# Picking source rows two tiles at a time, with the second scores a quarter later, in a three-layer graph transformer

## The chip, the cores and the metric

The kernel runs on one core of a Trainium2 chip. The core has TensorE (matmul, "PE"; its weight loads are "PEld"), VectorE ("DVE"), ScalarE ("ACT"), GpSimd ("POOL") and SyncE ("SP", which here only issues DMAs). The engines run side by side, each working through its own instructions in order; semaphores make one wait for another. TensorE writes to PSUM, which has eight banks of 2 KB in each of 128 partitions. The metric is device time in microseconds, lower is better.

## The reference

The input is a graph of 6250 nodes with 64 features and 206,250 directed edges sorted by their end node, each with 64 features of its own. Three layers of one-head attention over the incoming edges follow one another, then a softmax and a last normalization:

```python
q = x @ Wq + bq; k = x @ Wk + bk; v = x @ Wv + bv; e = edge_attr @ We
alpha = sum(q[dst] * (k[src] + e)) / sqrt(64)
w = softmax of alpha over the edges of one dst
x = relu(segment_sum((v[src] + e) * w, dst) + x @ Ws + bs)     # layer norm after layers 0 and 1
out = layernorm(x0 + log_softmax(x))
```

## The kernel before

Keys and values of a source node are linear in its features, so the kernel never builds them per edge. It brings the raw features `x[src]` of each edge next to the edge's own features, scores the 128-wide pair against a transformed query, sums the pairs with the softmax weights, and multiplies by Wv and We once per node.

Edges come in *chunks* of 768 (6 tiles of 128) whose end nodes lie within a window of 32 (`W`); four chunks make a *unit*, 67 full units and a short one. The chunks of a unit are four strips of 32 rows of one score matrix of 128 x 768. Scores, softmax and sums of a chunk go as partial results to DRAM (`tables`), and groups of four blocks of nodes are finished, as soon as their chunks are through, by a generator `finish` whose steps are advanced by `close_up`. This is the *node work*: combining the partials, the projection, the norm, and query and skip of the next layer (`project`). In layers 1 and 2 `close_up` is called in a unit's first quarter alone.

The rows `x[src]` come in two ways. Some tiles are gathered by indirect DMAs on GpSimd (line 601), released ahead of time by small copies on ScalarE (`gate`, line 633). The others are *picked* on TensorE (class `Picker`). Edges were sorted within their chunk in layer 0 so that all edges of a tile half draw from one stretch of eight blocks of nodes. A one-hot matrix (`hot`, line 1335, VectorE) picks the partition by matmul (line 1387, eight matmuls of 128x256 a tile pair; what is called a picked tile here is one tile position of two chunks, with four candidate blocks each, and fills one PSUM bank of 512 columns, tag `x`, of which there are two). Of the four candidates VectorE keeps the right one: a copy (line 1356) and three predicated copies (line 1359), `evacuate`. In layers 1 and 2 a unit has seven picked tiles, four for the first pair of chunks and three for the second, and `evacuate` is issued right behind the matmuls of its tile. `swap` (ScalarE, line 1346) exchanges the halves of a pair's tiles once all of them are there.

All five engines have a schedule written out by hand: instructions go to each engine in the order in which the code issues them. The loop over units (line 1904) goes through four *quarters* j = 0..3. In unit u the features of unit u are transposed (`turn`, lines 1679 and 1682), scores, softmax and weights of unit u-1 are made, unit u-2 is summed, and the tiles of unit u+1 are picked. In layers 1 and 2 the order is:

- before the quarters: `sums(u-2)` (line 1746, then a ScalarE copy), first half of the scores of u-1 (line 1692, bank `s`);
- quarter 0: `turn(0)`; the first maximum (`most`, line 1706, VectorE); the second half of the scores, bank `m`; one picked tile; the second maximum and behind it the exponential (line 1720, ScalarE); another picked tile; node work; requests for the queries of u+1 (line 1633, SP);
- quarter 1: `turn(1)`, two picked tiles;
- quarter 2: transposes of the first half of the probabilities (`weights`, line 1734, bank `p`, copied by line 1737), `turn(2)`, two picked tiles, transposes of the second half, the mask of u+1 and the first of its four loads of edge features (line 1659; the others follow at later turns);
- quarter 3: `turn(3)`, one picked tile, four stores of the partial results of u-2 (line 1757, SP); at the end the eight one-hot instructions for unit u+2.

The queries are written to one DRAM table `qq` (line 1442) and read from it with an offset known at run time (line 1633).

## Time and profile before

| | us |
|---|---|
| timed runs, median of 3 | 4206.91 (4202.07 to 4214.05) |
| the profiled execution | 4197.44 |
| its span, first to last instruction | 4195.7 |
| busy: PE / DVE / ACT / POOL | 3513.2 / 3452.3 / 2347.5 / 2563.3 |

In rows by line, `x7392 | 1084.9, 294` means 7392 instructions, 1084.9 us in which at least one was under way, 294 ns mean length; what follows is the idle time of the engine just before them and what ended it. Matmuls overlap one another, so the mean length is more than the distance from one to the next. In timeline rows the first number is the start in us, the second the length of a merged run of like instructions. In rows by stretch the columns are length, busy time of PE, PEld, DVE, ACT and POOL with instruction counts, the mean granted TensorE clock (1.00 is full rate), the share of the DMA engines in use, and GB/s.

### The profile page before, as it was taken

The numbers are of one execution on the slowest core, as the hardware profiler recorded it, in microseconds if no ns is written. First come the engines' busy times: TensorE is split into PE (matmuls) and PEld (weight loads), VectorE is DVE, ScalarE is ACT, GpSimd is POOL, SyncE is SP. The second block draws the span as 40 slices with busy tenths as digits, with TensorE's granted clock in tenths as the row PEclk, the third lists the DMA queues.
The fourth block names the chain that finished last, engine by engine and source line by source line (L and its number), as shares of the span: only waits on it lengthen the run. The fifth ranks groups of instructions, "written<-read, shape, count | busy, mean of one in ns | idle before, by whom it ended". The sixth has DMA issues, their size and how long they took to land.

```text
span 4195.7 us, 109920 instructions
## 1 busy us (share of the span) xinstructions
PE 3513.2 (84%) x35239; PEld 2484.7 (59%) x35239; DVE 3452.3 (82%) x12154; ACT 2347.5 (56%) x5994; POOL 2563.3 (61%) x2510
## 2 busy tenths in 40 slices
PE   3878889998998998895988888888858888888886
PEld 2445555555555555553767667666647667666674
DVE  5678898889888898874888888888758888888886
ACT  0445555655565555563655555555535656666665
POOL 5466666666666666663766666666447666666662
PEclk9899999999999999996999999999979999999998
DMA  5666666667666667665777777777648777777774
GB/s 109 177 165 180 174 186 177 175 181 187 179 176 181 178 173 183 180 182 130 189 182 183 182 176 178 192 176 182 164 127 192 185 174 185 187 179 183 179 179 101
DMA packets 779286, 729.02 MB, mean 174 GB/s; under 512 B 483080, under 2 KB 607938, under 8 KB 778704
## 3 DMA queue, kind: packets, MB, share of 16 engines
q1 hardware_dynamic: 630436, 512.79, 49.9%
q0 software_dynamic: 80000, 82.08, 10.2%
q10 hardware_dynamic: 68268, 127.03, 8.4%
q8 instruction: 288, 4.72, 0.5%
q14 instruction: 294, 2.41, 0.2%
HBM read 562.78 MB, written 158.68 MB: 172 GB/s over the span
## 4 chain that ended last, share of the span: by engine, by line


## 5 line engine op out<-in xcount | busy, mean ns | idle before, releaser
L601 POOL DMA_INDIRECT feat<-x,gate x1328 | 1318.0, 992 | 729.0 <-ACT gate L633 356.4
L601 POOL DMA_INDIRECT feat<-in_x,gate x1100 | 1172.1, 1066 | 690.4 <-ACT gate L633 369.6
L1387 PE MATMUL ps_x<-parts,hot 128*128 128x256 f32 x7392 | 1084.9, 294 | 223.1 <-DVE feat L1359 185.9
L1387 PEld LDWEIGHTS ps_x<-parts,hot 128*128 128x128 f32 x7392 | 946.0, 193 | 383.0 <-issue 213.5
L1682 ACT COPY featT<-ps_a 64x384 f32<-64x384 f32 x1588 | 753.8, 475 | 372.9 <-PE ps_a L1679 351.5
L1359 DVE COPY_PREDICATED feat<-which,ps_x 128x128 f32<-128x128 int32 x2772 | 838.0, 302 | 95.5
L1335 DVE TENSOR_SCALAR hot<-keys,rank 128x512 fp32r<-128x512 f16 (+1 forms) x1304 | 507.3, 457 | 4.7 <-DMA keys<-keyS 4.7
L1074 DVE TENSOR_SCALAR hit<-ruler,pos 128x384 bf16<-128x384 f16 x1608 | 456.3, 325 | 6.3 <-PE ps_m L1094 5.4
L1679 PE MATMUL ps_a<-ident,feat 128*128 128x128 f32 x2380 | 420.9, 286 | 40.7 <-DMA feat<-x,src_b 31.9
L1679 PEld LDWEIGHTS ps_a<-ident,feat 128*128 128x128 f32 x2380 | 279.6, 145 | 226.0 <-issue 185.3
L1356 DVE COPY feat<-ps_x 128x128 f32<-128x128 f32 x924 | 263.9, 286 | 173.6 <-PE ps_x L1387 166.4
L1692 PE MATMUL ps_s<-featT,q 128*32 128x384 f32 x2134 | 289.5, 507 | 81.4 <-DMA featT<-eaS 43.1
L1720 ACT ACTIVATE prob<-prob,part 128x768 f32<-128x768 f32 x204 | 190.3, 933 | 232.0 <-DVE part L1719 200.5
L1746 PE MATMUL ps_g<-feat,probT 128*32 128x128 f32 x9672 | 311.7, 275 | 2.4 <-ACT probT L1737 2.4
L1085 PE MATMUL ps_x<-hit,raw 128*64 128x384 bf16 x1608 | 294.5, 362 | 0.5 <-DVE hit L1074 0.4
L1746 PEld LDWEIGHTS ps_g<-feat,probT 128*32 128x32 f32 x9672 | 261.9, 110 | 25.6 <-ACT probT L1737 4.1
L1085 PE MATMUL ps_x<-hit,rest 128*64 128x384 bf16 x1608 | 276.2, 340 | 0.0
L1085 PE MATMUL ps_x<-hit,end 128*64 128x384 bf16 x1608 | 275.6, 339 | 0.0
L1737 ACT COPY probT<-ps_p 128x384 f32<-128x384 f32 x399 | 191.8, 481 | 124.7 <-PE ps_p L1734 92.8
L1734 PE MATMUL ps_p<-ident,prob 128*128 128x128 f32 x1197 | 206.8, 283 | 9.7 <-ACT prob L1720 9.6
L1118 ACT COPY eT<-ps_x 128x384 f32<-128x384 f32 x268 | 129.3, 483 | 122.1 <-PE ps_x L1085 84.7
L1136 ACT COPY feat<-ps_a 128x384 f32<-128x384 f32 x256 | 122.1, 481 | 133.6 <-PE ps_a L1128 97.4
(266 smaller groups left out, 5167.9 us busy)
## 6 DMA issues: line engine op xcount, KB each, us to landing
featT<-eaS SPq DMA_DIRECT2D x792, 192.0 KB
feat<-eaP SPq DMA_DIRECT2D x134, 768.0 KB
keys<-keyS SPq DMA_DIRECT2D x132, 448.0 KB
raw<-in_ea SPq DMA_DIRECT2D x536, 96.0 KB
eaS<-eT ACTq DMA_DIRECT2D x134, 384.0 KB
eaP<-feat ACTq DMA_DIRECT2D x128, 384.0 KB
shade<-maskS SPq DMA_DIRECT2D x198, 192.0 KB
feat<-x,gate POOLq DMA_INDIRECT x1328
```

What stands on the lines that cost most here:

```text
L601: nc.gpsimd.indirect_dma_start(out=feat[:, c, t, 0], out_offset=None, in_=xts[layer][:, :], in_offset=bass.IndirectOffsetOnAxis(ap=index[: ...
L1074: nc.vector.tensor_scalar(hit, ruler, self.pos[:, at : at + 1], None, ALU.is_equal)
L1085: nc.tensor.matmul(self.px[j * D : (j + 1) * D, :HE], self.parts[2 * h + i].thirds[part][:, j, t * D : (t + 1) * D], self.hits[h, 2 * i + ...
L1335: nc.vector.tensor_scalar(hot[:, h], keys[self.layer, k][:, first : first + n], rank[:, h : h + 1], None, ALU.is_equal)
L1356: nc.vector.tensor_copy(found, px[:, :, 0])
L1359: nc.vector.copy_predicated(found, which[:, first : first + 2, b].bitcast(I32).unsqueeze(2).to_broadcast([P, 2, D]), px[:, :, b],)
L1387: nc.tensor.matmul(px[:, v].rearrange("p b d -> p (b d)"), hot[:, h, (2 * pair + v) * P : (2 * pair + v + 1) * P], those[:, i, b0 + h * KB ...
L1679: nc.tensor.transpose(pt[:, t * P : (t + 1) * P], rows[:, 2 * t * D : 2 * (t + 1) * D], ident)
L1682: nc.scalar.copy(featT[:, :, h, :], pt[h * D : (h + 1) * D, : n * P].rearrange("d (i e) -> d i e", e=P))
L1692: nc.tensor.matmul(p_s[rows, :w], self.q[:, rows], self.featT[j][:, cols], start=True, stop=True)
L1734: nc.tensor.transpose(p_t[:, t, :n], self.prob[:n, at : at + P], ident[:n, :n])
L1746: nc.tensor.matmul(p_g[rows, :].rearrange("n (h d) -> n h d", h=2), self.probT[:, t, rows], batch[:, j, t], start=(t == 0), stop=(t == sel ...
```

## The change

In layers 1 and 2 the picked tiles are taken two positions at a time (`picks`, with a room of 2): sixteen matmuls into a PSUM tile of two adjoining banks, then one copy and three predicated copies for both. A unit has four such steps (two, two, two and one tile), one in each quarter. Two of the double tiles take four banks, so layers 1 and 2 run with a new PSUM pool: tag `s` serves the first scores and the first weights, `p` the sums, the second scores and the second weights, `a` the turns and the node work. Layer 0 keeps single tiles and its banks.

In all layers the sums of u-2 are issued in two pieces, three tiles before the first scores of u-1 and three behind, and the stores of the partial results in two halves, in quarters 1 and 3. In layers 1 and 2 the second scores are issued in quarter 1 behind `turn(1)`, and the second maximum, with the exponential, behind quarter 1's picked pair. All four loads of a unit's edge features are issued in quarter 2 of the unit before; the fourth has a buffer of its own. Query table and skip table get one copy for each layer (the skip table in the same way as `qq`). For units without a stored mask (three in layer 0 and the short one) the decoding of the mask (`uncode`) moves from the request to the third quarter of its own unit. The class `Line` learns to sum up to a given tile and to store one half.

```diff
--- before.py
+++ after.py
...
@@ -524,10 +523,17 @@
     nodes = ctx.enter_context(tc.tile_pool(name="nodes", bufs=2))
     early = ctx.enter_context(ExitStack())
     sorts = early.enter_context(tc.tile_pool(name="sorts", bufs=2))
+    psum = [early.enter_context(tc.tile_pool(name="psum0", bufs=1, space=bass.MemoryType.PSUM))]
     stock = [early.enter_context(tc.tile_pool(name="picks0", bufs=2))]
 
-    def ps(tag):
-        return psum.tile([P, 512], F32, tag=tag, name=f"ps_{tag}", bufs={"a": 2, "x": 2}.get(tag, 1))
+    bank_of = {"node": "g", "s0": "s", "s1": "s", "w0": "p", "w1": "p"}
+
+    def ps(use):
+        tag = bank_of.get(use, use)
+        wide = 2 if len(psum) > 1 and tag == "x" else 1
+        return psum[-1].tile(
+            [P, wide * 512], F32, tag=tag, name=f"ps_{tag}", bufs={"a": 2, "x": 2}.get(tag, 1)
+        )
 
     U0 = LEAD[0]
     STEP = -(-(N - WB * P) // (NW - 1))
...
@@ -697,7 +703,7 @@
     tables = [dram.tile([(NB + 1) * P, R], F32, name=f"part{h}") for h in range(2)]
     empty = const.tile([P, R], F32, name="empty")
 
-    qq = dram.tile([P, (NB + 1) * P], F32, name="qq")
+    qq = [dram.tile([P, (NB + 1) * P], F32, name=f"qq{i}") for i in range(L)]
     eps = const.tile([P, 1], F32, name="eps")
 
     def locate(k, m):
...
@@ -1351,55 +1358,65 @@
 
             if not self.late:
                 return
-            k, pair, t, px, which = self.late.pop()
-            found = loaded[self.layer, k][:, 2 * pair : 2 * pair + 2, t, 0]
-            nc.vector.tensor_copy(found, px[:, :, 0])
-            first = t * LB + 2 * pair
+            k, pair, t, m, px, which = self.late.pop()
+            found = loaded[self.layer, k][:, 2 * pair : 2 * pair + 2, t : t + m, 0]
+            which = which.rearrange("p (t c) b -> p c t b", c=LB)[:, 2 * pair : 2 * pair + 2, t : t + m]
+            px = px.rearrange("p t c b d -> p c t b d")
+            nc.vector.tensor_copy(found, px[:, :, :, 0])
             for b in range(1, KB):
                 nc.vector.copy_predicated(
                     found,
-                    which[:, first : first + 2, b].bitcast(I32).unsqueeze(2).to_broadcast([P, 2, D]),
-                    px[:, :, b],
+                    which[:, :, :, b].bitcast(I32).unsqueeze(3).to_broadcast([P, 2, m, D]),
+                    px[:, :, :, b],
                 )
-            if t == self.plan[k][pair] - 1:
-                self.swaps.append((k, pair, t + 1))
+            if t + m == self.plan[k][pair]:
+                self.swaps.append((k, pair, t + m))
 
         def flush(self):
 
             self.evacuate()
             self.swap()
 
+        def picks(self, k):
+
+            room = 2 if self.layer else 1
+            return [
+                (pair, t, min(room, most - t))
+                for pair, most in enumerate(self.plan.get(k, ()))
+                for t in range(0, most, room)
+            ]
+
         def batch(self, k):
 
-            for pair, most in enumerate(self.plan.get(k, ())):
-                for t in range(most):
-                    if not self.layer:
-                        self.swap()
-                    self.aim()
+            for pair, t0, m in self.picks(k):
+                if not self.layer:
+                    self.swap()
+                self.aim()
+                bank = "x" if self.layer else "pssp"[self.quarter]
+                px = ps(bank)[:, : m * 512].rearrange("p (t c b d) -> p t c b d", t=m, c=2, b=KB)
+                for t in range(t0, t0 + m):
                     at, hot = self.hots[k, t]
-                    bank = "x" if self.layer else "pssp"[self.quarter]
-                    px = ps(bank).rearrange("p (s b d) -> p s b d", s=2, b=KB)
                     for v in range(2):
                         w = t * WT + v
                         those, b0 = parts[w // HALF], w % HALF * WB
                         for h in range(NH):
                             for i in range(2):
                                 nc.tensor.matmul(
-                                    px[:, v].rearrange("p b d -> p (b d)"),
+                                    px[:, t - t0, v].rearrange("p b d -> p (b d)"),
                                     hot[:, h, (2 * pair + v) * P : (2 * pair + v + 1) * P],
                                     those[:, i, b0 + h * KB : b0 + (h + 1) * KB, :].rearrange("p b d -> p (b d)"),
                                     start=(h == 0 and i == 0),
                                     stop=(h == NH - 1 and i == 1),
                                 )
-                    self.late.append((k, pair, t, px, self.which[k]))
                     if not any(t < more for more in self.plan[k][pair + 1 :]):
                         self.free.append(self.hots.pop((k, t))[0])
-                    if self.layer:
-                        due = len(self.swaps)
-                        self.evacuate()
-                        self.swap(len(self.swaps) - due)
-                    self.aim()
-                    yield
+                self.late.append((k, pair, t0, m, px, self.which[k]))
+                if self.layer:
+                    due = len(self.swaps)
+                    self.evacuate()
+                    self.swap(len(self.swaps) - due)
+                self.aim()
+                yield
             self.which.pop(k, None)
 
     def late():
...
@@ -1612,6 +1629,11 @@
             self.mask = tos.tile([P, CE], BF16, name="shade")
             to = self.mask
             nc.sync.dma_start(to[:n, :], places[self.c : self.c + self.m].rearrange("c b e -> (c b) e"))
+
+        def uncode(self):
+
+            n = self.m * (BITS + 1)
+            to = self.mask
             for cols in self.halves:
                 w = cols.stop - cols.start
                 pc = ps("a")
...
@@ -1640,14 +1662,18 @@
             self.featT = []
             if not self.placed:
                 self.cover()
-            self.more()
+            for _ in range(self.m if self.layer else 1):
+                self.more()
 
         def more(self):
 
             j = len(self.featT)
             if j == self.m:
                 return
-            self.featT.append(work.tile([P, CE], F32, name="featT", bufs=6))
+            if self.layer and j == LB - 1:
+                self.featT.append(stock[0].tile([P, CE], F32, name="fourth", bufs=2))
+            else:
+                self.featT.append(work.tile([P, CE], F32, name="featT", bufs=6))
             if not self.plain:
                 self.turned(j, True)
 
...
@@ -1736,11 +1762,13 @@
                 self.probT = work.tile([P, TC, P], F32, name="probT", bufs=1)
             nc.scalar.copy(self.probT[:, t0 : t0 + m, :n], p_t[:, :, :n])
 
-        def sums(self):
-
-            p_g = ps("g")[:, :P]
+        def sums(self, first, upto):
+
+            if not first:
+                self.summed = ps("g")[:, :P]
+            p_g = self.summed
             batch = loaded[self.layer, self.k]
-            for t in range(self.tiles):
+            for t in range(first, upto):
                 for j in range(self.m):
                     rows = slice(j * W, (j + 1) * W)
                     nc.tensor.matmul(
@@ -1750,10 +1778,13 @@
                         start=(t == 0),
                         stop=(t == self.tiles - 1),
                     )
-            nc.scalar.copy(self.part[: self.rows, :P], p_g[: self.rows, :])
-
-        def store(self):
+            if upto == self.tiles:
+                nc.scalar.copy(self.part[: self.rows, :P], p_g[: self.rows, :])
+
+        def store(self, half=None):
             for j in range(self.m):
+                if half is not None and j // 2 != half:
+                    continue
                 nc.sync.dma_start(
                     tables[(self.c + j) % 2][ds(self.b[j], W), :], self.part[j * W : (j + 1) * W, :]
                 )
...
@@ -1904,13 +1947,13 @@
         for u in range(NU - 2):
             this = chunks[layer, u]
             picking = picker.batch(u + 1)
-            n = picked(layer, u + 1)
-            n //= 2
+            n = len(picker.picks(u + 1))
             pace = 0 if layer else 6 if u < 3 else 3
             while not opened:
                 move(1)
+            line.sums(u - 2, HT)
+            line.products(u - 1, 0)
             line.sums(u - 2)
-            line.products(u - 1, 0)
             if waiting:
                 active.append(waiting.pop(0))
             for j in range(LB):
@@ -1923,15 +1966,17 @@
                 free(u, j)
                 if j == 0 and layer:
                     line.most(u - 1, 0)
-                    line.products(u - 1, 1, "m")
+                if j == 1 and layer:
+                    line.products(u - 1, 1)
                 if j == 1:
+                    line.begun()
                     if not layer and placed(0, u + 1):
                         line.most(u - 1, 1)
                 a, b = -(-n * j // LB), -(-n * (j + 1) // LB)
                 if layer:
                     for i in range(max(b - a, 1)):
                         next(picking, None)
-                        if not i and not j:
+                        if not i and j == 1:
                             line.most(u - 1, 1)
                 if j == 0:
                     close_up()
@@ -1955,6 +2000,8 @@
                         chunks[layer, u + 1].across()
                 if j == 2:
                     line.weights(u - 1, 1)
+                    if not this.placed:
+                        this.uncode()
                     decode(layer, u + 2)
                     if placed(layer, u + 1):
                         chunks[layer, u + 1].across()
@@ -1980,6 +2027,8 @@
             lacking.extend(range(NW))
             if not layer:
                 early.close()
+                psum.append(ctx.enter_context(tc.tile_pool(name="psum", bufs=1, space=bass.MemoryType.PSUM)))
+                bank_of.update({"g": "p", "node": "a", "s1": "p", "w0": "s"})
                 stock[0] = ctx.enter_context(tc.tile_pool(name="picks", bufs=2))
                 parts.append(stock[0].tile([P, 2, HALF * WB, D], F32R, name="parts", bufs=1))
         u = NU - 2
...
```

74 lines of the change are left out of this document (43 added, 31 removed).

## The prediction

> **What bounds the kernel now.** I read the page first, then the busy time by stretch, the starts of one line that runs once in each unit, and the timeline of a unit without side work. Layers 1 and 2 hold what the change rewrites: the picked tiles of line 1387 and their copies.
>
> ```profile
> PE 3513.2 (84%) x35239; PEld 2484.7 (59%) x35239; DVE 3452.3 (82%) x12154; ACT 2347.5 (56%) x5994; POOL 2563.3 (61%) x2510
> ...
> L1387 PE MATMUL ps_x<-parts,hot 128*128 128x256 f32 x7392 | 1084.9, 294 | 223.1 <-DVE feat L1359 185.9
> ...
> L1359 DVE COPY_PREDICATED feat<-which,ps_x 128x128 f32<-128x128 int32 x2772 | 838.0, 302 | 95.5
> ```
>
> Over the span TensorE is busiest. Each picked unit has 56 picking matmuls (7 tiles of 8), so 7392 of them are 132 units, all in layers 1 and 2. Next, two stretches by engine (length, then busy us of TensorE, its weight loads, VectorE, ScalarE, GpSimd, then granted clock, DMA share, GB/s): one quiet unit, with no node work, and 700 us of layer 1.
>
> ```profile
> 2022.08:2035.68 13.60, 12.45 (x140) 10.44 (x140) 12.18 (x43) 8.69 (x24) 10.28 (x11) 1.00 0.79 193
> 2200.00:2900.00 700.00, 604.58 (x6149) 487.20 (x6148) 594.05 (x2076) 402.81 (x1038) 424.61 (x430) 0.98 0.73 181
> ```
>
> The quiet unit takes 13.60 us with TensorE at 12.45 and VectorE at 12.18: two engines nearly full, neither alone the bound. The softmax exponential of line 1720 runs once a unit, so its first and last starts give the mean unit:
>
> ```profile
> L1720 ACT ACTIVATE prob<-prob,part x64: 934/937/942, 2008.5 to 3012.9; 128x768 f32<-128x768 f32 x64
> ...
> L1720 ACT ACTIVATE prob<-prob,part x64: 935/937/940, 3140.6 to 4129.8; 128x768 f32<-128x768 f32 x64
> ```
>
> (3012.9-2008.5)/63 = 15.94 us in layer 1, (4129.8-3140.6)/63 = 15.70 in layer 2; mean 15.82. Now the timeline of quiet units (start, length, engine, line, operation). The reader is to see the order within each engine, and who hands over to whom.
>
> ```profile
> 2036.53 0.19 ACT L1720 ACTIVATION_READ_ACCUMULATOR prob<-prob,part 128x1 f32 x1
> ...
> 2038.03 0.49 PE L1734 MATMUL ps_p<-ident,prob 128*128 128x128 f32 x3
> ...
> 2038.60 2.29 PE L1387 MATMUL ps_x<-parts,hot 128*128 128x256 f32 x16
> ...
> 2040.72 0.49 PE L1734 MATMUL ps_p<-ident,prob 128*128 128x128 f32 x3
> ...
> 2041.30 1.19 PE L1387 MATMUL ps_x<-parts,hot 128*128 128x256 f32 x8
> ...
> 2042.42 1.52 PE L1746 MATMUL ps_g<-feat,probT 128*32 128x128 f32 x48
> 2042.53 0.29 DVE L1356 COPY feat<-ps_x 128x128 f32<-128x128 f32 x1 [0.20 <-PE ps_x L1387]
> ...
> 2042.85 0.98 DVE L1359 COPY_PREDICATED feat<-which,ps_x 128x128 f32<-128x128 int32 x3
> ...
> 2043.76 0.83 PE L1692 MATMUL ps_s<-featT,q 128*32 128x384 f32 x8
> 2043.87 2.98 DVE L1335 TENSOR_SCALAR hot<-keys,rank 128x512 fp32r<-128x512 f16 x8
> ...
> 2044.51 0.55 PE L1679 MATMUL ps_a<-ident,feat 128*128 128x128 f32 x3
> ...
> 2044.99 0.85 PE L1692 MATMUL ps_m<-featT,q 128*32 128x384 f32 x8
> ...
> 2045.77 2.16 PE L1387 MATMUL ps_x<-parts,hot 128*128 128x256 f32 x16
> ...
> 2046.77 0.54 DVE L1706 CUSTOM_DVE_ANT_0 prob<-ps_s,shade 128x384 f32<-128x384 f32 x1
> ...
> 2047.25 0.28 DVE L1356 COPY feat<-ps_x 128x128 f32<-128x128 f32 x1
> ...
> 2047.78 0.49 PE L1679 MATMUL ps_a<-ident,feat 128*128 128x128 f32 x3
> 2048.44 0.61 DVE L1706 CUSTOM_DVE_ANT_0 prob<-ps_m,shade,most 128x384 f32<-128x384 f32 x1
> ...
> 2049.28 0.94 ACT L1720 ACTIVATE prob<-prob,part 128x768 f32<-128x768 f32 x1 [1.99 <-DVE part L1719]
> ```
>
> The order is that of the code. On VectorE the second maximum (2048.44) stands right behind the copies of the first picked tile (2047.25); the exponential follows at 2049.28. In a unit's third quarter TensorE transposes its result (line 1734, at 2038.03), long after the exponential and its accumulator read ended at 2036.53+0.19 = 2036.72: three picked tiles lay between, and nobody waited. That slack is what the change spends.
>
> **The change part by part.** *Two tiles copied together.* 28 copies a unit become 16. A single tile's four take 2042.53 to 2043.83, 1.30 us. Price by element:
>
> ```profile
> L1511 DVE TENSOR_TENSOR w<-w 128x512 f32<-128x512 f32 x8 | 5.5, 692 | 0.3
> ...
> L1533 DVE TENSOR_TENSOR vb<-vb,sk 128x256 f32<-128x256 f32 x8 | 3.4, 424 | 0.3
> ```
>
> From 256 to 512 elements an instruction gains 692-424 = 268 ns, 1.05 ns an element; 128 more elements cost 134 ns. No row shows the two-bank form; it lies between no extra (1.30 us for four) and double (2.60). I take 1.30+4x0.134 = 1.83, as the copies are per-element work like those rows. VectorE then needs 3x1.83+1.30 = 6.8 instead of 7x1.30 = 9.1 us a unit: 2.3 us off VectorE. TensorE keeps its 56 matmuls.
>
> *Second scores and second maximum a quarter later.* In the second quarter the code now issues: tile transposes, second scores, 16 picking matmuls; on VectorE the pair's copies, and only then the second maximum; on ScalarE the exponential. The next thing in TensorE's queue is the third quarter's transposes of the probabilities. So from the end of the second quarter's picking TensorE stands still for the whole chain: 0.11 to the first copy (as from 2042.42 to 2042.53), 1.83 copies, 2049.28-2048.44 = 0.84 maximum to exponential, then exponential to the end of its read, 2036.72-2035.68 = 1.04 (the preceding exponential started one 13.60 us unit before 2049.28), some 0.01 more. **3.83 us, every unit.** Nothing covers it: in layers 1 and 2 node work is issued in the first quarter alone. Behind the waiting transposes are queued the third quarter's tile transposes, 16 picking matmuls and all that follows. With the copies' bounds the gap is 3.3 to 4.6 us.
>
> *The unit after.* TensorE start to start: sums 1.34 (2042.42 to 2043.76; in two pieces, the same 48 matmuls), first scores 0.75, first transposes 0.48, second transposes 0.48 the same, second scores 0.78 (2044.99 to 2045.77), three pairs at 2.06 (between 2.01 at 2045.77 and 2.12 at 2038.60) = 6.18, probabilities and tile transposes 0.57 (2038.03 to 2038.60) and 0.58 (2040.72 to 2041.30), last tile 1.12. Sum 12.28; with the gap 16.11. Does VectorE hold it up elsewhere? The first pair starts 2.57 us into the unit; its first one-hot tile (two of the eight instructions that take 2.98 us from 2043.87) is ready at 2.2, the second at 2.9 when 3.6 is due: no. The first pair's copies end at 6.7, the second pair's matmuls at 7.95: no, and 1.3 us of VectorE lie free for node work. Quiet unit: **16.11 against 13.60**.
>
> *Node work and loads.* Before, a mean unit is 15.82-13.60 = 2.22 above the quiet one. After, VectorE's part of node work falls into idle time; TensorE's stays on the path. Its rows for 43 units:
>
> ```profile
> L1537 PE MATMUL ps_g<-ve,wT 128*128 128x64 f32 x64 | 9.4, 294 | 8.3 <-DVE skip L1448 8.3
> L1437 PE MATMUL ps_a<-xT,eq 64*128 64x512 f32 x16 | 9.0, 641 | 0.0
> L1446 PE MATMUL ps_g<-ws,xT 64*128 64x65 f32 x64 | 8.8, 278 | 0.0
> L1515 PE MATMUL ps_a<-ident,w 128*128 128x128 f32 x32 | 5.0, 278 | 0.0
> L1432 PE MATMUL ps_a<-ident,y 128*64 128x128 f32 x31 | 4.7, 272 | 0.0
> ```
>
> 36.9/43 = 0.86 us; I add 0.2 for clashes on the two banks these outputs now share with the tile transposes: 1.06. The loads of the edge features go out together in the third quarter of the unit before, and the query table gets one copy a layer, so these waits of the same 700 us should go, and no longer cost anything:
>
> ```profile
> PE ps_x L1387 <- DVE feat L1359: 52.1, 62, 1.8
> PE ps_s L1692 <- DMA featT<-eaS: 19.7, 13, 3.1
> ...
> SPq L1633 <- DMA qq<-qs: 48.4, 8, 6.3
> ```
>
> SP's queue keeps its number of DMAs. Half the stores move from the fourth quarter to the second; they wait for a copy of sums that are issued at the unit's start, and behind them on SP stand loads that are needed only in the next unit. GpSimd's gathers are released by copies whose place does not change.
>
> *Clock.* What does a gap of 3.83 us do to the clock? Two gaps of layer 1, and the stretches behind them:
>
> ```profile
> 2102.87 2.02 PE L1692 MATMUL ps_s<-featT,q 128*32 128x384 f32 x4 [3.70 <-DMA featT<-eaS]
> ...
> 2470.09 2.32 PE L1692 MATMUL ps_s<-featT,q 128*32 128x384 f32 x4 [2.97 <-DMA featT<-eaS]
> ```
>
> ```profile
> 2100.00:2102.87 2.87, 0.00 (x0) 0.00 (x0) 1.47 (x5) 0.00 (x0) 2.13 (x2) 0.77 0.59 127
> 2102.87:2110.00 7.13, 7.13 (x34) 3.88 (x34) 1.54 (x6) 2.09 (x6) 5.57 (x6) 0.61 0.55 137
> ...
> 2470.00:2476.00 6.00, 5.91 (x30) 2.89 (x31) 1.14 (x4) 2.09 (x6) 1.65 (x3) 0.72 0.48 94
> ```
>
> Behind 2.97 us of idle the clock was 0.72 over 6 us: 1.7 us of full clock lost. Around 3.70 us it was 0.77 already inside the gap and 0.61 over the 7.13 us behind: 2.8 lost. So 0 to 2.8 a unit (0 would need this not to recur). I take 1.8, near the smaller row, since dense picking follows my gap where single scores with 1.9 us more of waits and half-rate work followed those.
>
> The Trainium skill ("TensorE: Matmul & The Clock Gate", Part 1) has TensorE drop to half rate after one idle free-running window of about 3.4 us. By that rule alone a 3.83 us gap holds a whole window in some 12% of units, an estimate from the page of 0.2 us a unit and 4410 us in all, against 4620 by the rows. The trace goes further than the page: 2.97 us sufficed.
>
> *The rest.* Layer 0 keeps single tiles and its banks; sums around the scores reorder the same matmuls (nothing; -20 to +10 us). Layer tails share banks (a few us more) but wait less for masks: nothing, within 15.
>
> *Sum.* 16.11+1.06+1.8 = 18.97 against 15.82: +3.15 us, times 132 = +416. The profiled execution took 4197.44 (span 4195.7), 9.5 below the median 4206.91 and below the lowest timed run. Against its own time 4613; on the median's scale about **4620**.
>
> **The rivals.** *The clock stays up:* +1.35 a unit, +178: 4385. The Trainium skill's rule above would put the time beside this case. For it: gaps follow dense work. Against: both gaps above.
>
> *The clock is lost as behind the 3.70 us gap:* 2.8 instead of 1.8, +132 more: 4755. For: its length is the nearest to 3.83. Against: there TensorE went on in single scores.
>
> *Faster: the gap doesn't form.* If the second maximum did not stand behind the second pair's copies, its 0.84 and the exponential's 1.04 would hide behind 2.06 us of picking; then a unit is 12.28+1.06 = 13.34, -2.48, times 132 = -327: 3880. For: VectorE's lighter load is real, 52.1 us of TensorE's waits in that stretch are for these copies. Against: the code issues copies first, and the timeline shows VectorE taking a maximum only after the copies issued before it. It decides below 2.48 us of gap and lost clock together.
>
> **How the numbers follow.** Gap with about one clock loss (4480 to 4720): 0.6; clock stays up: 0.18; larger loss: 0.12; no gap: 0.08; gains and losses meet: 0.02. The likeliest gives 4620. The range, 4370 to 4770, takes in both clock cases. Slower by over 0.3% (13 us, about what this measurement can tell): 0.90; within: 0.02; faster: 0.08.
>
> **What would show it.** Right: 396+132 = 528 copies of one kind; a TensorE wait on the exponential before line 1734's transposes near 3.8 us in nearly every unit of layers 1 and 2, ScalarE's exponential starting behind a maximum that starts behind the pair's last predicated copy; a quiet unit of 17 to 18 us; a granted clock under 0.9 in both layers; VectorE's busy time down by about 260 us; the waits for edge features and for the query table gone; layer 0 unchanged. Wrong: exponential ended before the second pair's last matmul; clock at 0.97 or more; a pair's copies far from 1.83 us.

## The result and the profile after

Over four executions each, on the same chip, the changed kernel takes 4529.35 us (4525.71 to 4531.18) and the kernel before 4210.48 us (4202.07 to 4223.55). The ratio is 1.0761 [1.0735, 1.0787]: slower by 7.6%. The forecast was 4620 us with a range of 4370 to 4770. The profiled execution of the changed kernel took 4530.92 us, with a span of 4529.2, against 4197.44 before: 333 us more.

From the page of the changed kernel: busy time by engine, the granted TensorE clock in 40 slices, and three groups (line, engine, operation, tiles, count | busy us, mean ns | idle us before them and its releaser).

```profile
PE 3617.2 (80%) x35239; PEld 2688.7 (59%) x35239; DVE 3214.5 (71%) x10570; ACT 2366.7 (52%) x5994; POOL 2578.6 (57%) x2510
...
PEclk9899999999999999978888888888788888888887
...
L1365 DVE COPY feat<-ps_x 128x256 f32<-128x256 f32 (+1 forms) x528 | 202.8, 384 | 839.6 <-PE ps_x L1404 837.0
...
L1367 DVE COPY_PREDICATED feat<-which,ps_x 128x256 f32<-128x256 int32 (+1 forms) x1584 | 649.4, 410 | 54.3
L1760 PE MATMUL ps_s<-ident,prob 128*128 128x128 f32 (+1 forms) x417 | 112.6, 401 | 533.2 <-ACT prob L1746 533.2
```

VectorE's busy time fell from 3452.3 to 3214.5 us, and its share from 82% to 71%, as the joint copies were to do. TensorE issues the same 35239 instructions, but its share fell from 84% to 80%, and from the 18th slice on, where layer 1 begins, the clock is at 7 or 8 tenths where it was mostly at 9. One group holds the idle time: the transposes of the probabilities (line 1760) waited 533.2 us for ScalarE's exponential of line 1746. The predicated copies (line 1367), the largest VectorE group, still take 649.4 us, in 1584 instructions. The clock and the transposes in the kernel before, for comparison:

```profile
PEclk9899999999999999996999999999979999999998
...
L1734 PE MATMUL ps_p<-ident,prob 128*128 128x128 f32 x1197 | 206.8, 283 | 9.7 <-ACT prob L1720 9.6
```

The waits of TensorE between 2200 and 2900 us (engine, tile and line, what it waited for: us in total, times, longest), where before the copies of picked tiles and the loads of edge features headed the list; its first line is now

```profile
PE ps_s L1760 <- ACT prob L1746: 146.1, 37, 4.7
```

The copies and the loads are no longer among the waits, and 146.1/37 = 3.95 us a unit stands in their place. Now one quiet unit of the changed kernel. The timeline is of its second and third quarter (start, length, engine, line, operation, in brackets the wait before it):

```profile
2039.36 0.42 DVE L1365 COPY feat<-ps_x 128x256 f32<-128x256 f32 x1 [0.93 <-PE ps_x L1404]
2039.81 1.39 DVE L1367 COPY_PREDICATED feat<-which,ps_x 128x256 f32<-128x256 int32 x3
...
2041.10 0.61 DVE L1732 CUSTOM_DVE_ANT_0 prob<-ps_p,shade,most 128x384 f32<-128x384 f32 x1
...
2041.94 0.93 ACT L1746 ACTIVATE prob<-prob,part 128x768 f32<-128x768 f32 x1 [4.20 <-DVE part L1745]
...
2042.78 0.19 ACT L1746 ACTIVATION_READ_ACCUMULATOR prob<-prob,part 128x1 f32 x1
...
2043.02 0.61 PE L1760 MATMUL ps_s<-ident,prob 128*128 128x128 f32 x3 [3.71 <-ACT prob L1746]
...
2043.92 3.43 PE L1404 MATMUL ps_x<-parts,hot 128*128 128x256 f32 x16
...
2050.97 0.55 PE L1705 MATMUL ps_a<-ident,feat 128*128 128x128 f32 x3
...
2051.28 2.14 PE L1404 MATMUL ps_x<-parts,hot 128*128 128x256 f32 x16
```

This is the chain that the prediction had worked out, link by link: picked pair, copy 0.42, three predicated copies 1.39, and only then the second maximum at 2041.10; the exponential at 2041.94, its accumulator read, and at 2043.02 the transposes, for which TensorE stood still for 3.71 us. The 16 picking matmuls that follow take 3.43 us; the next pair, at 2051.28, takes 2.14. The same place by stretch (length, busy us of TensorE, its weight loads, VectorE, ScalarE and GpSimd, then granted clock, DMA share, GB/s), with one whole quiet unit and the 700 us of layer 1 that the prediction used:

```profile
2024.66:2041.94 17.28, 13.58 (x138) 11.87 (x138) 10.45 (x30) 8.88 (x24) 12.86 (x14) 0.90 0.61 162
2043.00:2047.00 4.00, 3.98 (x21) 3.98 (x22) 0.00 (x0) 2.73 (x7) 2.56 (x4) 0.57 0.96 259
2047.00:2056.50 9.50, 9.50 (x119) 7.91 (x118) 8.03 (x23) 5.03 (x14) 7.21 (x8) 1.00 0.44 117
2200.00:2900.00 700.00, 549.78 (x5272) 476.93 (x5272) 444.54 (x1333) 350.12 (x890) 369.21 (x371) 0.86 0.61 156
```

The clock is 0.57 for the 4 us behind the gap and 1.00 again in the next 9.5 us: 4 x 0.43 = 1.7 us of full clock lost for one gap. The whole unit takes 17.28 us where it took 13.60. The mean unit comes from the exponential's first and last start in each layer:

```profile
L1746 ACT ACTIVATE prob<-prob,part x64: 934/934/936, 2007.4 to 3182.3; 128x768 f32<-128x768 f32 x64
...
L1746 ACT ACTIVATE prob<-prob,part x63: 934/934/936, 3311.1 to 4448.8; 128x768 f32<-128x768 f32 x63
```

That is (3182.3-2007.4)/63 = 18.65 us in layer 1 and (4448.8-3311.1)/62 = 18.35 in layer 2, 18.50 in the mean where it was 15.82. The 2.68 us more, over the 125 intervals counted here, are 335 us: the whole of the 333 that the profiled execution lost. Layer 0 gave and took nothing: layer 1's first counted exponential starts at 2007.4, and did at 2008.5.

### The profile page after: what moved, and what is told of

It reads as the page before. It is cut to its first block, busy times and chain, and to the rows that moved or that the text cites. A ratio compares the mean times of both kernels' runs of the same rounds, so it can differ in the third digit from the quotient of the medians.

```text
span 4529.2 us, 107247 instructions
## 1 busy us (share of the span) xinstructions
PE 3617.2 (80%) x35239; PEld 2688.7 (59%) x35239; DVE 3214.5 (71%) x10570; ACT 2366.7 (52%) x5994; POOL 2578.6 (57%) x2510
## 4 chain that ended last, share of the span: by engine, by line
## 5 line engine op out<-in xcount | busy, mean ns | idle before, releaser
L1404 PE MATMUL ps_x<-parts,hot 128*128 128x256 f32 x7392 | 1193.8, 322 | 0.0
L1404 PEld LDWEIGHTS ps_x<-parts,hot 128*128 128x128 f32 x7392 | 1096.1, 225 | 82.6 <-DVE feat L1365 43.1
L1365 DVE COPY feat<-ps_x 128x256 f32<-128x256 f32 (+1 forms) x528 | 202.8, 384 | 839.6 <-PE ps_x L1404 837.0
L1708 ACT COPY featT<-ps_a 64x384 f32<-64x384 f32 x1320 | 626.8, 475 | 169.6 <-PE ps_a L1705 154.9
L1367 DVE COPY_PREDICATED feat<-which,ps_x 128x256 f32<-128x256 int32 (+1 forms) x1584 | 649.4, 410 | 54.3
L1760 PE MATMUL ps_s<-ident,prob 128*128 128x128 f32 (+1 forms) x417 | 112.6, 401 | 533.2 <-ACT prob L1746 533.2
L1760 PEld LDWEIGHTS ps_s<-ident,prob 128*128 128x128 f32 (+1 forms) x417 | 61.9, 191 | 564.0 <-ACT prob L1746 560.5
L1774 PE MATMUL ps_p<-feat,probT 128*32 128x128 f32 x6600 | 235.8, 276 | 11.9 <-DVE most L1732 9.2
L1774 PEld LDWEIGHTS ps_p<-feat,probT 128*32 128x32 f32 x6600 | 179.7, 110 | 84.6 <-issue 50.9
L1763 ACT COPY probT<-ps_p 128x384 f32<-128x384 f32 (+1 forms) x269 | 129.3, 481 | 192.4 <-PE ps_p L1760 165.5
```

The costliest lines, as they stand in the source:

```text
L1365: nc.vector.tensor_copy(found, px[:, :, :, 0])
L1367: nc.vector.copy_predicated(found, which[:, :, :, b].bitcast(I32).unsqueeze(3).to_broadcast([P, 2, m, D]), px[:, :, :, b],)
L1404: nc.tensor.matmul(px[:, t - t0, v].rearrange("p b d -> p (b d)"), hot[:, h, (2 * pair + v) * P : (2 * pair + v + 1) * P], those[:, i, b0 ...
L1708: nc.scalar.copy(featT[:, :, h, :], pt[h * D : (h + 1) * D, : n * P].rearrange("d (i e) -> d i e", e=P))
L1774: nc.tensor.matmul(p_g[rows, :].rearrange("n (h d) -> n h d", h=2), self.probT[:, t, rows], batch[:, j, t], start=(t == 0), stop=(t == sel ...
```

## The experiments

**Theory:** the second maximum stands on VectorE behind the copies of the second quarter's pair, so exponential and transposes come one after the other behind the picking, TensorE waits 3.7 to 3.95 us in every unit, and its clock falls behind each wait. **Rivals:** the new layout of the banks makes pieces wait that did not before; steps of two tiles are too coarse, whatever their order; the clock has another cause than the wait.

The first four runs shared a chip on which the kernel before took 4203.19 us (4192.06 to 4218.63, nine executions). In the diffs, `-` is the changed kernel of this document unless another is named.

### e1: the second maximum ahead of the pair

```diff
                 if layer:
+                    if j == 1:
+                        line.most(u - 1, 1)
                     for i in range(max(b - a, 1)):
                         next(picking, None)
-                        if not i and j == 1:
-                            line.most(u - 1, 1)
```

> The second maximum is issued ahead of quarter 1's picked pair instead of behind it; all else as changed. Theory (the gap: maximum and exponential stand behind the pair's copies, and TensorE's next work needs them): the exponential now runs beside the pair's sixteen matmuls. VectorE is still busy with the first pair's copies until about 0.9 us before the second pair's matmuls end, so about 1.05 us of the gap stays in a quiet unit, too short to lose the clock as a rule: quiet unit 13.1 us, mean unit 14.2 to 14.8, total 3980 to 4080 us. Rival 1 (shared banks: sums, second scores and second weights queue for one bank): the banks are the same, so it stays at 4450 or more. Rival 2 (coarse steps: sixteen matmuls against one set of copies leave both engines idle in turn): the steps are the same, 4450 or more.

It took 4185.98 us, ratio 0.997 [0.9953, 0.9988]: one call moved ahead of a loop takes back all of the loss and a little more, with the same banks and the same steps of two tiles. So neither layout nor step is what the time was lost to. The size was missed by 100 us. A quiet unit of this run, and the stretch of layer 1:

```profile
2032.30:2045.29 12.99, 12.07 (x140) 10.33 (x138) 10.46 (x30) 8.69 (x24) 9.94 (x11) 1.00 0.78 208
2200.00:2900.00 700.00, 602.34 (x6363) 515.12 (x6354) 536.90 (x1616) 419.81 (x1077) 454.21 (x447) 0.95 0.71 187
```

The wait in that stretch:

```profile
PE ps_s L1760 <- ACT prob L1746: 88.0, 42, 4.0
```

and its exponential in layer 1 (duration, then first and last start):

```profile
L1746 ACT ACTIVATE prob<-prob,part x65: 932/935/937, 2006.4 to 2986.6; 128x768 f32<-128x768 f32 x65
```

The quiet unit is 12.99 us where 13.1 was expected, with 0.92 us of the wait left in it, and below the 13.60 of before. But over the stretch the wait is still 88.0/42 = 2.1 us and the clock 0.95, and the mean unit is (2986.6-2006.4)/64 = 15.32. VectorE's timeline in a unit with node work shows why:

```profile
2205.13 1.22 DVE L1525 TENSOR_TENSOR w<-both,mm 128x1024 f32<-128x1024 f32 x1
...
2206.38 0.69 DVE L1528 TENSOR_TENSOR w<-w 128x512 f32<-128x512 f32 x1
...
2206.99 0.61 DVE L1732 CUSTOM_DVE_ANT_0 prob<-ps_p,shade,most 128x384 f32<-128x384 f32 x1
```

The node work (lines 1525 and 1528), issued in the first quarter, now stands ahead of the second maximum in place of the copies. The prediction's rival without a gap left this out, and its 3880 us were too low for it.

### e2: the transposes later

The other end of the chain. The exponential stays late, and what waits for it moves behind the third quarter's picked pair.

```diff
-                if j == 2:
+                if j == 2 and not layer:
                     line.weights(u - 1, 0)
                 this.turn(j)
...
                 if j == 2:
+                    if layer:
+                        line.weights(u - 1, 0)
                     line.weights(u - 1, 1)
```

> Maximum and exponential stay where the change put them; the transposes of the first half of the probabilities move on TensorE from ahead of quarter 2's turn to behind its picked pair. Theory: the chain of 3.8 us runs beside the turn and sixteen matmuls (2.3 us) of quarter 2; what is left of the gap is about 1.5 us, or none where the engine lags; mean unit 14.3 to 15.2, total 4000 to 4130 us. Rivals (shared banks, coarse steps): 4450 or more.

4148.01 us, ratio 0.9875 [0.9857, 0.9892]: faster than both kernels, though 18 us above the expected range. The waits of the stretch:

```profile
PE ps_s L1760 <- ACT prob L1746: 71.1, 44, 2.1
PE ps_p L1774 <- ACT probT L1763: 46.6, 43, 1.1
```

The stretch itself:

```profile
2200.00:2900.00 700.00, 580.79 (x6303) 501.08 (x6306) 534.40 (x1598) 414.62 (x1065) 443.98 (x442) 0.99 0.71 185
```

and one quiet unit's transposes in the timeline:

```profile
2045.63 0.55 PE L1760 MATMUL ps_s<-ident,prob 128*128 128x128 f32 x3 [1.51 <-ACT prob L1746]
```

The wait for the exponential fell to 71.1/44 = 1.6 us, with the clock at 0.99. A new wait of 46.6/43 = 1.1 us stands beside it: the sums now wait for ScalarE's copies of the transposed weights, which run later too. This new wait is what the expectation had not priced in. In the quiet unit the first wait is 1.51 us, and it leaves the clock up.

### e3: the gap filled with work

Does the wait cost the clock, or something else? Thirteen matmuls of the identity with itself, written into the tile that the transposes then overwrite, fill the gap. They are useless work; the result stays the same.

```diff
+            if self.layer and not h and self.c // LB < NU - 3:
+                for _ in range(13):
+                    nc.tensor.matmul(p_t[:, 0, :], ident, ident, start=True, stop=True)
             for t in range(m):
                 at = (t0 + t) * P
                 nc.tensor.transpose(p_t[:, t, :n], self.prob[:n, at : at + P], ident[:n, :n])
```

> Thirteen matmuls of the identity with itself are put on TensorE ahead of the first transposes of the probabilities, into the same bank, which the transposes overwrite: about 3 us of work without use inside the gap. The wait for the exponential stays. Theory: granted clock in layers 1 and 2 goes from 0.86 to 0.97 or more, quiet unit from 17.3 to 15.9, total 4340 us (4310 to 4400): the clock's own share of the loss, 1.4 us a unit. If the clock is lost for another reason or does not set the time: 4500 to 4600.

4295.77 us, ratio 1.0224 [1.0189, 1.0259], a little below the expected range. A kernel with more to do is faster than the changed one. The quiet unit and the stretch:

```profile
2036.22:2051.97 15.75, 14.93 (x167) 13.23 (x165) 10.46 (x30) 8.69 (x23) 12.09 (x13) 1.00 0.73 189
2200.00:2900.00 700.00, 653.85 (x7002) 572.59 (x7001) 494.27 (x1486) 387.55 (x999) 424.05 (x414) 1.00 0.67 173
```

The chain's place in the timeline of the quiet unit and the one behind it:

```profile
2049.18 3.06 PE L1760 MATMUL ps_s<-ident 128*128 128x128 f32 x26
...
2051.97 0.94 ACT L1746 ACTIVATE prob<-prob,part 128x768 f32<-128x768 f32 x1 [4.29 <-DVE part L1745]
...
2053.05 0.55 PE L1763 MATMUL ps_s<-ident,prob 128*128 128x128 f32 x3 [0.81 <-ACT prob L1746]
...
2053.69 2.14 PE L1404 MATMUL ps_x<-parts,hot 128*128 128x256 f32 x16
...
2055.67 0.49 PE L1763 MATMUL ps_p<-ident,prob 128*128 128x128 f32 x3
```

The clock is 1.00 throughout. The chain is unchanged: from the fill's start at 2049.18 to the transposes at 2053.05 it is 3.87 us, of which 0.81 remain as a wait. So what separates this run from the changed kernel is the clock: (1.0761-1.0224) x 4210 = 226 us, over 132 units 1.7 us each, the same 1.7 that the stretch behind one gap showed. The remaining 2.2% is what the chain costs beyond what VectorE's lighter load saves.

### e5: single tiles in the new order

```diff
-            room = 2 if self.layer else 1
+            room = 1
```

> Layers 1 and 2 pick single tiles again (seven a unit: two, two, two, one in the quarters), in the changed order and banks; the second maximum stands behind quarter 1's first tile, ahead of its second. Theory: the gap is one tile's copies 1.30, maximum 0.84, exponential 1.04 and 0.1, less the second tile's matmuls 1.07: 2.2 us; TensorE 12.1+2.2 and part of the clock loss: quiet unit about 15.3, total 4290 to 4400 us. Rival 2 (coarse steps): back to the 4210 us of before or under it. Rival 1 (banks): 4450 or more.

4484.09 us, ratio 1.0672 [1.0654, 1.069]: above what was expected. What TensorE waited for in the stretch:

```profile
PE ps_s L1760 <- ACT prob L1746: 121.1, 39, 4.5
```

The transposes of one quiet unit in the timeline, with the wait ahead of them, and the picking behind:

```profile
2046.75 0.55 PE L1760 MATMUL ps_s<-ident,prob 128*128 128x128 f32 x3 [1.97 <-ACT prob L1746]
...
2047.55 3.52 PE L1404 MATMUL ps_x<-parts,hot 128*128 128x256 f32 x16
```

The 4 us behind that wait, and the stretch:

```profile
2047.00:2051.00 4.00, 4.00 (x23) 4.00 (x22) 1.21 (x4) 2.73 (x7) 3.09 (x4) 0.57 1.01 267
2200.00:2900.00 700.00, 564.26 (x5449) 481.86 (x5448) 526.11 (x1846) 363.04 (x921) 382.45 (x382) 0.88 0.62 161
```

The wait is still that for the exponential, 121.1/39 = 3.1 us in the mean; in the quiet unit it is 1.97, since one tile's copies stand ahead of the maximum instead of two tiles'. What was mispriced is the clock: the 4 us behind this wait ran at 0.57, as in the changed kernel, and the 16 matmuls there took 3.52 us. The length of the wait does not decide it alone. One unit earlier the same wait left the clock at 1.00, and the 16 matmuls behind it took 2.14 us:

```profile
2031.63 0.55 PE L1760 MATMUL ps_s<-ident,prob 128*128 128x128 f32 x3 [1.95 <-ACT prob L1746]
...
2032.26 2.14 PE L1404 MATMUL ps_x<-parts,hot 128*128 128x256 f32 x16
```

Of the ten waits of 1.95 to 1.97 us between 2005 and 2900 us, seven were followed by 4 us at 0.57 to 0.68 and three by 4 us at 1.00. Both units shown also have a wait of some 0.7 us for a copy, 4 us before this one, so the 1.97 us are not all of their idle time; what decides between them is not shown. With single tiles the new order still costs 6.7%, so the joint copies are not what it is lost to.

### e7: the late maximum in the kernel before

The remaining runs were made on two other chips, where the kernel before itself took 5458.60 us (5416.12 to 5508.37) and 5486.03 us (5438.46 to 5507.49); each ratio is to the kernel before on the same chip. Here the kernel before gets one line of the change's order and nothing else (`-` is the kernel before):

```diff
-                        if not i and not j:
+                        if j == 1 and i == b - a - 1:
                             line.most(u - 1, 1)
```

> The kernel before with one line moved: the second maximum (with the exponential) goes from behind quarter 0's first picked tile to behind quarter 1's last. Single tiles, all banks and loads as before. Theory: a wait of one tile's copies, maximum and exponential (1.30+0.84+1.04+0.1 = 3.3 us) opens ahead of quarter 2's transposes, and costs 1.5 us of clock on top; TensorE's other waits for copies vanish: quiet unit about 17, total 4520 us (4430 to 4610). If banks or pairs made the loss: within 60 us of 4203.

5910.05 us, ratio 1.0839 [1.0775, 1.0902]; 1.075 was expected. TensorE's waits between 2600 and 3300 us:

```profile
PE ps_p L1734 <- ACT prob L1720: 102.1, 22, 10.8
```

With the old banks, single tiles, old scores and old loads, the place of the second maximum alone makes the wait and, on this chip, a loss of 8.4%, of the size of the whole change's on the first chip.

### e8: both ends of the chain mended

The edits of e1 and e2 together, once on each of the two chips.

> Both moves together on the changed kernel: the second maximum ahead of quarter 1's pair, and the first transposes of the probabilities behind quarter 2's pair. Theory: no wait for the exponential is left in a quiet unit, and few elsewhere; TensorE alone sets 12.1 us, with its node work and some waits for the copies of the weights: quiet unit 12.2 to 13.0, mean 13.7 to 14.6, total 3930 to 4050 us. If either alone already had all there is to win: 4140 to 4190.

> Both moves together, as in e8_both, whose call ran on a chip on which the kernel before took 5459 us. The ratio there was 0.959. Theory: the waits that the moves take away are the kernel's own, so the ratio holds or improves where little else stalls: 3980 to 4060 us against about 4205. If the gain belonged to that chip's stalls: 4140 or more, as with either move alone.

5229.13 us, 0.9591 [0.9535, 0.9648], and on the other chip 5242.80 us, 0.9565 [0.9519, 0.9611]. This is the best version found: about 4% below the kernel before. TensorE's waits for the exponential between 2100 and 3000 us, in the second of the two runs:

```profile
PE ps_s L1760 <- ACT prob L1746: 2.4, 6, 1.0
```

On these chips layer 0 still runs in the first 280 us or so of this window. Over the whole run the first transposes (into `ps_s`) stood idle for the exponential for 40.6 us, 0.3 us a unit, where the changed kernel had 533.2: nearly all of the wait is gone. It was not run on the chip of the first group, so its time there is open.

### e4 and e9: the scores back in the first quarter

e4 undoes the move of the second scores and of the second maximum and keeps all else; e9 adds e2's later transposes to it.

```diff
                 if j == 0 and layer:
                     line.most(u - 1, 0)
-                if j == 1 and layer:
                     line.products(u - 1, 1)
...
-                        if not i and j == 1:
+                        if not i and not j:
                             line.most(u - 1, 1)
```

> Undoes one part alone: second scores, second maximum and exponential go back to quarter 0 (scores behind the first maximum, the maximum behind the first picked pair, ahead of the node work). Two-tile copies, shared banks, split sums and early loads stay. Theory (the place of the second maximum makes the loss): what is left of the wait is about 1 us in a quiet unit, as with the maximum put ahead of the pair (12.95), but node work on VectorE no longer stands ahead of the maximum: mean unit 14.2 to 14.9, total 3990 to 4090 us. Rival 1 (shared banks) and rival 2 (coarse steps): no better than 4186, the time with the maximum ahead of the pair.

> Second scores, maximum and exponential back in quarter 0, as in e4_scores_back (ratio 1.037 on the chip with the long times). First theory, unchanged: mean unit 14.2 to 14.9, 3990 to 4090 us. Second theory, from that run: with the second scores in quarter 0 they need the bank of the sums, which ScalarE must have copied, and the wait of the transposes stays short; if something else in that order stalls, 4200 to 4360 us, and the profile shows it as a wait other than on the exponential.

> Second scores, maximum and exponential in quarter 0 and the first transposes of the probabilities behind quarter 2's pair: the exponential has a whole pair's time of slack. Theory: as both moves together or a little better, since node work stands behind the maximum: 3950 to 4050 us. If the order with the scores in quarter 0 stalls for another reason: 4150 to 4350 us.

Both missed: e4 took 5655.14 us, 1.0368 [1.0306, 1.043], and 5666.65 us, 1.0322 [1.0276, 1.0368]; e9 took 5665.18 us, 1.0321 [1.0275, 1.0366]. The waits for the exponential between 2100 and 3000 us, of e4 and then of e9, on the same chip:

```profile
PE ps_s L1760 <- ACT prob L1746: 37.9, 20, 7.4
```

```profile
PE ps_s L1760 <- ACT prob L1746: 0.5, 1, 0.5
```

e9 has next to none left (3.7 us ahead of the transposes into `ps_s` over the whole run, against 173.3 in e4 on the same chip) and is no faster than e4, so the exponential did not limit it there. Part of what did is in another kind of row: TensorE idle on "issue", waiting for nothing that the profile shows, ahead of its runs of small matmuls. The group of weighted sums, first in the kernel before on the first chip:

```profile
L1746 PE MATMUL ps_g<-feat,probT 128*32 128x128 f32 x9672 | 311.7, 275 | 2.4 <-ACT probT L1737 2.4
```

In e8, and then in e9, on the same other chip:

```profile
L1774 PE MATMUL ps_p<-feat,probT 128*32 128x128 f32 x6600 | 435.8, 303 | 370.3 <-issue 293.5
```

```profile
L1774 PE MATMUL ps_p<-feat,probT 128*32 128x128 f32 x6600 | 531.9, 328 | 535.6 <-issue 412.3
```

On the first chip the sums of the kernel before cost 275 ns each with 2.4 us of idle time in all; on the others a sum takes over 300 ns and hundreds of microseconds of "issue" stand ahead of them. e8 has 370.3 us of idle time there and e9 535.6, but that is 165 us of 437 between the two profiled spans (5670.4 and 5233.1). Another 235 us are TensorE's busy time, 4288.9 against 4053.6 for the same 35239 instructions, at a granted clock of 0.841 in e9 and 0.890 in e8. The second scores themselves are among what slowed down: written into bank `p` in the first quarter, right behind the sums and their stalls, they take 816 ns each in e9 and 513 in e8 (line 1718, those of `featT`), and they wait 44.2 us for ScalarE's copy of the sums out of that bank, where that row of e8 on the same chip has 0.0. Whether this is the whole reason why returning the scores costs more than it brings on these chips is not settled, and whether it would on the first chip is open too.

### e6: one table a layer in the kernel before

The kernel before with one copy of query and skip table for each layer (`qq` and `skS` as lists, indexed by layer), which is the change's smallest part.

> The kernel before with one query table and one skip table for each layer, and nothing else of the change. Theory: SP's stalls on the query table go (48 us of 700), and with them most of TensorE's 20 us of 700 on late edge features: 20 to 55 us faster, 4150 to 4185 us. If the loads are late for another reason (all four go out within 3 us of use): within 0.3% of 4203.

> The kernel before with a query and a skip table for each layer, as in e6_before_tables (ratio 1.004, 1.001 to 1.008, on the chip with the long times). Theory: 20 to 55 us faster than before, from the 20 us in 700 that TensorE waits for late edge features behind SP's stalls on the query table. If the loads are late because they go out within 3 us of use: within 0.3%.

5478.69 us, 1.0043 [1.0011, 1.0075], and 5507.32 us, 1.0042 [1.0013, 1.007]. The gain did not show; if anything 0.4% was lost. TensorE is held by "issue" on these chips, so a wait of the loads that is taken away there says little about the first chip, where the wait was read.

## Why the prediction was right, step by step

- **The gap.** 3.83 us predicted, 3.71 measured in the quiet unit and 3.95 in the mean of the stretch. It is where it was put, and every link of it is in the order given. e1, e2 and e7 show that the cause is the place of the maximum and of the transposes, not the banks.
- **The copies of a pair.** 1.83 us predicted from per-element prices; 0.42+1.39 = 1.81 by the rows of the timeline. Copies of one kind: 528, as counted. VectorE's busy time fell by 238 us where about 260 was said.
- **The clock.** 1.8 us a unit predicted from what followed a gap of 2.97 us; 1.7 measured behind one gap and by the fill over the whole run, and 1.53 between the two quiet units (17.28 against 15.75 in e3). The two gaps of before had 1.7 and 2.8; that the smaller was the better guide was a judgement, not worked out, and some luck is in it. The granted clock was 0.86 in the stretch. The Trainium skill ("TensorE: Matmul & The Clock Gate", Part 1) has the rate fall after one idle window of about 3.4 us, by which most of these gaps would have passed; the trace differs, since each of the 49 waits for the exponential between 2005 and 2900 us, 3.70 to 4.71 us long, was followed by 4 us at 0.64 or less, and in e5 seven of ten waits of 1.95 to 1.97 us were followed by 4 us at 0.68 or less.
- **TensorE's own pieces: mis-sized.** "Sum 12.28" was too high by 0.40. The quiet unit of e3 has 15.75-3.87 = 11.88 outside the chain. The pairs take 1.98 (2053.69 to 2055.67 in e3), not 2.06, three times a unit; the tile transposes ahead of the first pair take 0.31 (2050.97 to 2051.28 in the changed kernel), not 0.48. 11.88+3.71+1.7 = 17.29 comes to the quiet unit of 17.28 (or 11.88+3.87+1.53, with the chain counted as in e3); the prediction had 17.91.
- **Node work.** 1.06 us above the quiet unit predicted; 18.50-17.28 = 1.22 measured.
- **The number of units.** The excess was multiplied by 132. The steady intervals alone, 125 of them, make up the loss; the units at the ends of a layer together lost nothing. At 2.68 us each the other 7 would have been 19 us.
- **Side terms.** TensorE's waits for the edge features and SP's for the query table are gone from the stretch, and layer 0 is unchanged, as said; ScalarE's and GpSimd's busy time rose by 19 and 15 us.
- **The rivals.** Neither clock rival came, and the gap did form. The one without a gap named the right lever, and e1 pulled it: 343 us below the changed kernel, where 740 were worked out.

So the mechanism held in every step, and the forecast lay 91 us above the time: some 60 from the pieces of the mean unit (18.97 against 18.50, times 132), the rest from the units at the ends and from the two scales of time.

## What to carry to other kernels

When work moves to another place in a program whose engines run their queues in order, follow it link by link: behind what does it now stand on its own engine, and what stands behind its consumer on the consumer's engine? An engine that got 238 us lighter did not help, because one instruction of it had moved behind 1.8 us of copies and the next engine's queue was blocked behind the result. Mend both ends of such a chain, the producer earlier and the consumer later (here 0.997 and 0.9875 alone, about 0.96 together on other chips), and where a gap can't be avoided count the slow clock behind it as well.

## What was unexpected of the hardware

- The clock can fall behind waits shorter than the 2.97 and 3.70 us that the prediction had read in the trace of before, but not behind each: of ten waits of 1.95 to 1.97 us in e5 seven were followed by 4 us at 0.68 or less and three by 4 us at 1.00, while in e2 all 47 waits of 1.50 to 1.52 us between 2005 and 2900 us were followed by 1.00.
- Filling a wait with useless matmuls brought 226 us (e3 against the changed kernel).
- An instruction over two banks is cheaper than two over one, as these groups of VectorE in layers 1 and 2 of the changed kernel show by shape (the last column is the idle time ahead): 446 ns for 256 elements against 303 for 128 in the predicated copies, 419 against 279 in the plain ones, 1.1 ns for each element more.

```profile
L1367 DVE COPY_PREDICATED feat<-which,ps_x 128x256 f32<-128x256 int32 x1167 | 520.2, 446 | 39.9
...
L1365 DVE COPY feat<-ps_x 128x256 f32<-128x256 f32 x389 | 163.0, 419 | 804.4 <-PE ps_x L1404 802.6 <-issue 1.9
L1367 DVE COPY_PREDICATED feat<-which,ps_x 128x128 f32<-128x128 int32 x390 | 118.0, 303 | 13.4
...
L1365 DVE COPY feat<-ps_x 128x128 f32<-128x128 f32 x130 | 36.3, 279 | 7.5 <-PE ps_x L1404 6.8
```

- The same kernel took 4203 us on one chip and 5459 and 5486 us on two others, where TensorE stands on "issue" ahead of its small matmuls. A ratio from one chip need not hold on another: e7's loss, e8's gain, e4's loss and e6's missing gain were seen on those two alone.
